# A graph layer on one core: the last four plain quads summed by equality matrix, the last round's units on both PSUM rings

## The chip, the core and the metric

The kernel runs on one core of a Trainium2 chip. A core has five engines that run side by side and meet through semaphores: PE (TensorE, matmuls into PSUM; PEld is its loading of weights), DVE (VectorE), ACT (ScalarE), POOL (GpSimd) and SP (SyncE, which here only issues DMAs). Each engine takes its instructions in the order in which they stand in its queue. The metric is the device time of one execution in microseconds.

## The reference

A graph network layer with 6250 nodes of 128 features and 200000 edges. `src` is the node that an edge is summed into, `dst` the node that it reads; the edges are sorted by `dst`.

```python
h = jnp.maximum(_layernorm(x, axis=-1), 0.0)
xw = h @ W_in
W_ij = shifted_softplus(f_ij @ W_f1 + b_f1) @ W_f2 + b_f2
W_ij = W_ij * f_ij_cutoff
x_ij = xw[dst] * W_ij
out = jax.ops.segment_sum(x_ij, src, num_segments=6250)
return x + shifted_softplus(out @ W_o1 + b_o1) @ W_o2 + b_o2
```

Here `f_ij` has 20 numbers for each edge and `f_ij_cutoff` one. The sum over edges with the same `src` is what the change is about: the edges are not sorted by `src`, so each must be added to a row that can be anywhere.

## The kernel before

**Quads.** 512 edges, in four chunks of 128, are a quad; there are 391, numbered 0 to 390 (the last has three chunks). For each, PE makes the filter weights `W` and gathers the node rows `xg` with one-hot matmuls, ACT scales the rows by the cutoff (`xc`), and DVE multiplies both to the messages: 128 edges on the partitions, 4 x 128 numbers each.

**Three ways to sum messages by `src`.**

- *Permuted quads* (8, 10, ... 388, 191 of them): the messages are split in bf16 parts, sorted by matmuls with a permutation (`pq` to `mst`), and eight quads together, a *round*, are added to the SBUF table `accT` by matmuls with one-hots of the row (`unit_pe`: `un` from `mst` and the one-hots `so`, L838). A round has four units, one for each 128 slots of the sorted edges; a unit fills four PSUM banks, and `unit_evac` adds them to `accT` on DVE (L849). Edges that don't fit go through an overflow path: `over_row`, `over_eq`, `over_sum` (`orow`, `oeq`, `osum`), one scatter (`os`) for two quads. The last round has 7 quads.
- *Plain quads*: DVE makes an equality matrix of the `src` numbers in each chunk (`eq`, `s1_eq`), PE multiplies it with the messages (`pp`, `s3_pe`), so that all edges of one chunk with the same `src` carry the same sum; ACT copies that to SBUF (`s3_copy`), and indices are made that send all but one of equal rows to a trash row (`s3_idx`, `s3_ji`). Then POOL scatters each chunk with an indirect DMA that adds into DRAM (`acc`).
- *Listed quads*: no equality matrix for the sum. Ahead of time a list is made of those rows that occur more than once in a chunk (`l_eq`, `l_count`, `l_scan` and so on); the messages themselves are scattered, and the doubles go to rows of their own behind the table. Later these rows are loaded (`l_load`), summed by `src` (`over_row`, `l_same`, `l_sum`) and scattered once. A list covers 16 quads, made in groups of four; the last covers what is left.

Of the 200 quads that aren't permuted (`splain`), the first 12 are plain and the other 188 are listed, in 12 lists, the last with 12 quads. `listed` sets these bounds (LB and LE in the code).

**Accumulators.** Four tables in DRAM take the scatters in turn, so that a scatter need not wait for the one before. Table 0 is read back and added to `accT` while the last iterations run (`r0_tp`); scatters from then on go to tables 1 to 3.

**The order of work.** The body is one long program, written out in Python with no loop on the chip: iteration i calls fixed steps for quads i+1 to i-4, and steps put down in a table of hooks, keyed by iteration and point (`AT` gives for each its distance and its point in the iteration). A plain quad q has its equality matrix and its messages in iteration q+1, its sums in q+2, its indices in q+4, and is scattered in q+4; a listed quad is scattered in q+2. The units of the last round stand in iterations 393, 395, 397 and 399. The last list is summed from the iteration of its last quad plus LASTLAG = 5 on, or the next one without a unit.

**PSUM.** There are eight banks, in two rings of four. Ring A holds `z`, `xg` and `W` of the main path, ring B all else: `pp`, `pq`, `po`, `orow`, `osum`, `lsum`, and the units, which need all four banks of it.

**The exit and the tail.** Behind the body stands a test whether some list or gather overflowed. Two small matmuls (`fps`, on ring A, L1362) and four DVE instructions make a flag (`flagi`, L1365 to L1369); every engine loads it (L1372) and branches (L1373); here all engines meet. With these inputs the flag is 0. Instructions written behind the body can stand before others of the body in an engine's queue, and the other way round; the queues quoted below are what the chip gets. Then the tail: for 13 groups of 512 nodes, three accumulator tables are loaded (`ta_in`, L1458) and summed (POOL and DVE), transposed, added to `accT`, and taken through the two output matmuls. The rows of `x` that are added at the end are loaded near the end of the body, and the output bias is added to them on DVE (`x_bias`, 13 instructions, L1171).

Of the kernel before, what the change touches and what calls it, by code (L numbers as in the profile page):

```python
# [7 lines left out]
F32 = mybir.dt.float32  # L8
# [12 lines left out]
P = 128  # L21
# [30 lines left out]
SW = 16  # L52
LEARLY = 8
LLATE = 12
LLAG = 12
LASTLAG = 5
LCAP = 7
LFIRST = 3
LREST = 36
# [16 lines left out]
def tile_gnn(ctx: ExitStack, tc: tile.TileContext, x, fB, cT, srcT, srcr, srci, dstr, win_, wf1, wf2, bias, bo1c, wo1,  # L76
# [26 lines left out]
    rounds = unit_rounds(mpq)  # L103
    uslots = unit_slots(rounds)
    units = {i for us in uslots for i in us}
# [3 lines left out]
    plain = {q: n for n, q in enumerate(splain)}  # L109
    NS = len(splain)  # L110
    LB, LE = listed(NS) if spread else (0, 0)
    CE = min(128, EP // P) if spread else EP // P
    CB = min(4 * NS + 64, EP // P) if spread else 0
# [8 lines left out]
    wend = [splain[LB + SW * w + wsize[w] - 1] for w in range(NW)]  # L122
    wlag = [LLAG] * (NW - 1) + [LASTLAG]
    for w in range(NW):
# [13 lines left out]
    ps = edge.enter_context(tc.tile_pool(name="ps", bufs=2, space=PSUM))  # L138
# [275 lines left out]
    def l_base(w):  # L414
        return ACC_R + P * (NA - 1 - w if w < NA else NA + NW - 1 - w)
# [40 lines left out]
    def l_index(w):  # L456
# [4 lines left out]
        nc.vector.tensor_scalar(row, j, pre, None, op0=ALU.add)  # L461
        oh = sp_.tile([P, P + LCAP + 1], BF16, tag="loh", name="loh", bufs=1)
        nc.vector.tensor_scalar(oh[:, :P + LCAP], iotl, pre, None, op0=ALU.is_equal)
        bad = sp_.tile([P, 4 * SW], F32, tag="lbad", name="lbad", bufs=1)[:, :n]
        nc.vector.tensor_scalar(bad, row, float(P), None, op0=ALU.is_gt)
        nc.vector.scalar_tensor_tensor(bad, j, float(LCAP), bad, op0=ALU.is_gt, op1=ALU.max)
        nc.vector.tensor_scalar(row, row, float(l_base(w) - 1), None, op0=ALU.add)
# [8 lines left out]
    def l_id(w):  # L476
        n0 = 4 * (LB + SW * w)
        jd = lst.pop(("jd", w))
        own = sp_.tile([P, LCAP], F32, tag="lown", name="lown", bufs=1)
        n = 4 * wsize[w]  # L480
        t = wk.tile([P, 4 * SW], BF16, tag="lsel", name="lsel", bufs=1)[:, :n]
        for k in range(LCAP):
            nc.vector.scalar_tensor_tensor(t, jd, float(k + 1), srcT_sb[:, n0:n0 + n], op0=ALU.is_equal,
                                           op1=ALU.mult, accum_out=own[:, k:k + 1])
        two = sp_.tile([P, LCAP, 2], BF16, tag="ltwo", name="ltwo", bufs=1)
        nc.vector.tensor_copy(two[:, :, 0], own)
# [339 lines left out]
    un = {}  # L826

    def unit_pe(r, s):
        ts = []
        for g in range(4):  # L830
            t = ps.tile([P, 512], F32, tag="B", name="un", bufs=4)
            ts.append(t)
        qs = rounds[r]
        for q in qs:
            for k in range(3):
                for g in range(4):
                    v = slice(g * CAP, (g + 1) * CAP)
                    nc.tensor.matmul(ts[g][:, :GN], mp[q]["ms", s][v, k * P:(k + 1) * P], mp[q]["oh"][v],  # L838
                                     start=(q == qs[0] and k == 0), stop=(q == qs[-1] and k == 2))
        un[r, s] = ts  # L840
# [52 lines left out]
    with tc.manual_schedule():  # L893
# [115 lines left out]
        def at(i, point, fn, *a):  # L1009
            hooks.setdefault((i, point), []).append((fn, a))  # L1010

        def put(name, base, fn, *a, busy=()):
            d, point = AT[name]
            i = max(clear(base + d, busy) if busy else base + d, 0)
            at(i, point, fn, *a)
            return i
# [70 lines left out]
        busy = units | {prep_start(g) + k for g in range(1, NG) for k in range(5)}  # L1087
# [85 lines left out]
        if spread:  # L1173
            k = clear(mid + 9, busy, 2)
# [3 lines left out]
            k = clear(NQ - 1, busy, 2)  # L1178
# [25 lines left out]
        for r in range(-(-len(mpq) // RKQ)):  # L1204
# [5 lines left out]
            k = put("rk_count", i, rank_count, r, busy=units)  # L1210
            k = max(k + 1, i + AT["rk_own"][0])
            at(k, AT["rk_own"][1], rank_own, r)
            k = clear(max(k, i + AT["rk_over"][0]), units)
            at(k, AT["rk_over"][1], rank_over, r)
            k = max(k + 1, i + AT["rk_slot"][0])
# [5 lines left out]
        for w in range(NW):  # L1221
            for g in range(wsize[w] // 4):
# [9 lines left out]
                k = put("l_dup", i, l_dup, w, g)  # L1232
# [12 lines left out]
            k = clear(i + AT["l_sum"][0], units)  # L1245
# [4 lines left out]
            k = put("l_int", k, over_int, ("L", w))  # L1250
# [6 lines left out]
        for q in mpq:  # L1257
            put("pm", q, perm_oh, q)
            put("rem1", q, part_rem, q, 1)
            put("rem2", q, part_rem, q, 2)  # L1260
            put("ext", q, part_ext, q)
            if q + 4 in units:
                for s in range(4):
                    at(q + 3, "PE2", permute, q, s)
                for s in range(4):
                    at(q + 3, "PE2", perm_out, q, s)
            else:
                for s in range(4):
                    put(f"p{s}", q, permute, q, s)
                    put(f"o{s}", q, perm_out, q, s)  # L1270
            if mpi[q] % 2 or q == mpq[-1]:
                k = mpq[mpi[q] + 1] if mpi[q] + 1 < len(mpq) else q + 2
                put("over_pe", k, over_pe, q)
                put("over_out", k, over_out, q)
                put("over_idx", q, over_idx, q)
                put("over_dg", q, over_dg, q)
                k = put("over_row", q, over_row, q, busy=units)
                put("over_eq", k, over_eq, q)
                k = put("over_sum", q, over_sum, q, busy=units)
                put("over_copy", k, over_copy, q)  # L1280
                put("over_ji", k, over_ji, q)
                k = put("over_int", k, over_int, q)
                at(k, "S", over_scatter, q)
        last = mpq[-1]
        for r, us in enumerate(uslots):
            for s, k in enumerate(us):
                for h in range(3):
                    d, point = AT[f"so{h}"]
                    at(max(k + d, us[s - 1]) if s else k + d, point, unit_oh, r, s, h)
                put("unit", k, unit_pe, r, s)  # L1290
                put("evac", k, unit_evac, r, s)
# [81 lines left out]
    with tc.For_i(0, redo, 1):  # L1373
# [8 lines left out]
        with tc.For_i(0, trips, 1) as ci:  # L1382
# [39 lines left out]
            e = wk.tile([P, P], F32, tag="a", name="fe")  # L1422
# [15 lines left out]
            s = wk.tile([P, P], F32, bufs=1, tag="dg", name="fs")  # L1438
# [126 lines left out]
def unit_rounds(qs):  # L1565
    return [qs[r:r + RND] for r in range(0, len(qs), RND)]
# [23 lines left out]


def listed(ns):
    return (ns - LLATE - (ns - LEARLY - LLATE) // SW * SW) // 4 * 4, ns // 4 * 4


def unit_its(qs):
# [3 lines left out]
def clear(i, busy, n=1):  # L1600
    while any(i + k in busy for k in range(n)):
        i += 1
    return i
# [11 lines left out]
def prep_start(g):  # L1615
    busy = unit_its(sorted_quads(4 * PREP_GAP * (g + 8)))
    return clear(7 + PREP_GAP * (g - 1), busy, 2) - 1
# [100 lines left out]
```

## Time and profile before

| What | us |
|---|---|
| Three runs | 1917.09, 1922.52, 1920.89 (median 1920.89) |
| The profiled execution, its own time | 1917.92 |
| Its span in the profile | 1916.1 |
| PE busy | 1802.2 (94%) |
| DVE busy | 1655.1 (86%) |
| POOL busy | 1516.2 (79%) |
| ACT busy | 1475.0 (77%) |
| The first matmul of the last round's units starts at | 1839.03 |
| The last evacuation of a unit starts at | 1862.71 |
| The first load of the tail is issued at | 1866.01 |

Times within the execution are counted from the start of the span; the profiled execution's own time is 1.8 us more than its span. A busy PE is not a PE at its peak, since matmuls overlap. A line number is that of the kernel file; where several steps share a line, the names of the tiles tell them apart (`osum<-mo,oeq` is a matmul into `osum`). Some records of matmuls can be missing from a trace.

### The profile page before, as it was taken

How to read it: one execution, taken by the hardware profiler on the slowest of the kernel's cores; microseconds unless marked ns; L12 is line 12 of the kernel's file. 1: busy time of each engine (PE TensorE's matmuls, PEld its weight loads, DVE VectorE, ACT ScalarE, POOL GpSimd, SP SyncE). 2: the span in 40 equal slices, each digit the busy share in tenths (PEclk: the TensorE clock that was granted, in tenths of full speed). 3: DMA queues.
4: the chain of work that ended last, by engine and by line, in shares of the span. 5: the costliest groups of instructions: out<-in, count | busy, mean ns of one | idle time of the engine just before them, and what ended most of it. 6: DMA issues, size and time to landing. Idle time of an engine off the chain costs nothing. (4 is left out here: it accounts for less than half of the span.)

```text
span 1916.1 us, 58074 instructions
## 1 busy us (share of the span) xinstructions
PE 1802.2 (94%) x20601; PEld 1220.0 (64%) x20601; DVE 1655.1 (86%) x4692; ACT 1475.0 (77%) x4045; POOL 1516.2 (79%) x964
## 2 busy tenths in 40 slices
PE   3589999999999999999999999999999999999976
PEld 2456666666666666666666666666666666666654
DVE  5678899899999999999999889889889889898766
ACT  3578887778887878887887887887887787787725
POOL 3568777788887888888888888888888888888755
PEclk9799999999999999999999999999999999999997
DMA  7887786777776677776777767667667667667658
GB/s 268 200 178 163 150 194 123 137 129 126 141 134 122 117 139 127 131 144 127 128 132 126 129 116 136 123 118 132 123 121 130 122 125 128 121 114 135 109 104 264
DMA packets 351704, 267.56 MB, mean 140 GB/s; under 512 B 96719, under 2 KB 315258, under 8 KB 351410
## 3 DMA queue, kind: packets, MB, share of 16 engines
q1 hardware_dynamic: 218786, 197.43, 35.5%
q0 software_dynamic: 132336, 66.32, 34.8%
q8 instruction: 163, 2.67, 0.6%
q14 instruction: 131, 1.07, 0.2%
q10 hardware_dynamic: 288, 0.07, 0.0%
HBM read 154.65 MB, written 109.00 MB: 138 GB/s over the span
## 5 line engine op out<-in xcount | busy, mean ns | idle before, releaser
L637 POOL DMA_INDIRECT acc<-s,lji x751 | 1214.3, 1617 | 247.7 <-issue 175.5
L742 PE MATMUL pq<-pt,pm 128*128 128x387 bf16 x3056 | 581.8, 336 | 1.3 <-ACT s L595 0.6
L565 ACT ACTIVATE xc<-xg,cb 128x128 f32<-128x128 f32 x1564 | 448.0, 375 | 163.4 <-PE xg L552 142.6
L748 ACT CAST mst<-pq 128x387 bf16<-128x387 f32 x764 | 363.9, 487 | 91.9 <-PE pq L742 65.6
L560 PEld LDWEIGHTS W<-w,a 128*128 128x128 f32 x3128 | 420.3, 195 | 17.0 <-issue 5.9
L742 PEld LDWEIGHTS <-pm 128*128 128x128 bf16 x3056 | 294.0, 98 | 197.2 <-issue 4.0
L838 PE MATMUL un<-so,mst 32*128 32x392 bf16 x9168 | 408.9, 324 | 10.5 <-DVE rank L684 4.2
L560 PE MATMUL W<-w,a 128*128 128x128 f32 x3128 | 418.4, 277 | 0.0
L838 PEld LDWEIGHTS <-mst 32*128 32x128 bf16 x9168 | 245.5, 93 | 148.3 <-issue 19.7
L371 ACT ACTIVATE a<-a,con 128x512 f32<-128x512 f32 x391 | 282.5, 723 | 11.6
L731 DVE TENSOR_TENSOR pt<-pt 128x512 f32<-128x512 f32 x382 | 260.5, 682 | 0.0
L717 DVE TENSOR_SCALAR pm<-iotp,pos 128x576 bf16<-128x576 f16 x764 | 256.0, 395 | 0.0
L366 ACT ACTIVATE a<-z 128x512 f32<-128x512 f32 x391 | 236.4, 605 | 19.2 <-PE z L361 19.2
L849 DVE TENSOR_TENSOR accT<-un,accT 128x392 f32<-128x392 f32 x368 | 182.4, 557 | 62.5 <-PE un L838 33.0
L823 DVE TENSOR_SCALAR so<-iot,mst 128x392 bf16<-128x392 f16 x764 | 217.9, 335 | 1.9 <-PE un L838 1.9
L637 POOL DMA_INDIRECT acc<-os,oji x108 | 178.9, 1657 | 47.3 <-issue 13.9
L575 DVE TENSOR_TENSOR pt<-W,xc 128x512 f32<-128x512 f32 x191 | 131.3, 688 | 57.1 <-ACT xc L565 28.7
L361 PE MATMUL z<-ft,ws 123*128 123x512 bf16 x391 | 153.7, 394 | 27.7 <-DMA ft<-fsd 21.2
L575 DVE TENSOR_TENSOR s<-W,xc 128x512 f32<-128x512 f32 x188 | 128.5, 684 | 43.3 <-ACT xc L565 32.1
L552 PE MATMUL xg<-wn,oh 63*128 63x128 bf16 x1564 | 155.3, 220 | 10.9 <-DVE oh L378 6.5
L549 PE MATMUL W<-b2rep,onesb 64*128 64x512 bf16 x391 | 152.3, 389 | 0.0
L637 POOL DMA_INDIRECT acc<-s,ji x48 | 77.7, 1618 | 67.3 <-ACT ji L618 27.8
(215 smaller groups left out, 1787.5 us busy)
## 6 DMA issues: line engine op xcount, KB each, us to landing
rb<-reld SPq DMA_DIRECT2D x391, 64.0 KB
sb<-src SPq DMA_DIRECT2D x192, 128.0 KB
fsd<-f SPq DMA_DIRECT2D x49, 480.0 KB
ft<-fsd SPq DMA_DIRECT2D x195, 120.0 KB
fb<-in_fB_dram SPq DMA_DIRECT2D x49, 320.0 KB
ft<-fsd SPq DMA_DIRECT2D x195, 80.0 KB
wn<-tab SPq DMA_DIRECT2D x782, 15.8 KB
acc<-s,lji POOLq DMA_INDIRECT x751
```

The costliest lines, as they stand in the source:

```text
L366: nc.scalar.activation(a, st[q]["z"], AF.Exp)
L371: nc.scalar.activation(a, a, AF.Ln, bias=half, scale=0.5)
L560: nc.tensor.matmul(W[:, c, :], st[q]["a"][:, c * P:(c + 1) * P], w2, start=False, stop=(c == 3))
L565: nc.scalar.mul(xc[:, c, :], st[q]["xg"][:, c, :], late["c", q // CQ][:, 4 * (q % CQ) + c:4 * (q % CQ) + c + 1])
L575: nc.vector.tensor_tensor(m[:, :, :P], st[q]["W"], st[q]["xc"], op=ALU.mult)
L637: nc.gpsimd.indirect_dma_start(out=accs[k][:rows, :], out_offset=bass.IndirectOffsetOnAxis(ap=ji, axis=0), in_=s, in_offset=None, compute_ ...
L717: nc.vector.tensor_scalar(pm[:, c], iotp, rk[r]["pos"][:, 4 * j + c:4 * j + c + 1], None, op0=ALU.is_equal)
L731: nc.vector.tensor_tensor(pt[:, :, k * P:(k + 1) * P], a, high(a), op=ALU.subtract)
L742: nc.tensor.matmul(t[:, :PW], mp[q]["pm"][:, c, s * P:(s + 1) * P], high(mp[q]["pt"][:, c:c + 1, :PW])[:, 0], start=(c == 0), stop=(c == 3))
L748: nc.scalar.copy(mp[q]["ms", s][:, :PW], mp[q].pop(("q", s))[:, :PW])
L823: nc.vector.tensor_scalar(so, iotw[:, :GN], w[:, 3 * P // 2:3 * P // 2 + 1], None, op0=ALU.is_equal)
L838: nc.tensor.matmul(ts[g][:, :GN], mp[q]["ms", s][v, k * P:(k + 1) * P], mp[q]["oh"][v], start=(q == qs[0] and k == 0), stop=(q == qs[-1] a ...
```

## The change

```diff
+LTAIL = 4
...
     def unit_pe(r, s):
         ts = []
         for g in range(4):
-            t = ps.tile([P, 512], F32, tag="B", name="un", bufs=4)
+            t = ps.tile([P, 512], F32, tag="A" if r == len(rounds) - 1 and s % 2 else "B", name="un", bufs=4)
             ts.append(t)
...
                 k = put("over_row", q, over_row, q, busy=units)
-                put("over_eq", k, over_eq, q)
-                k = put("over_sum", q, over_sum, q, busy=units)
+                e = put("over_eq", k, over_eq, q)
+                k = clear(max(e, q + AT["over_sum"][0]), units)
+                at(k, AT["over_sum"][1], over_sum, q)
...
 def listed(ns):
-    return (ns - LLATE - (ns - LEARLY - LLATE) // SW * SW) // 4 * 4, ns // 4 * 4
+    return (ns - LLATE - (ns - LEARLY - LLATE) // SW * SW) // 4 * 4, ns // 4 * 4 - LTAIL
```

The last four of the quads that aren't permuted, 385, 387, 389 and 390, are plain instead of listed. The last list ends with quad 383 and has 8 quads in two groups; its sum starts in iteration 388 instead of 396. The second and fourth unit of the last round take their four banks from ring A, whose tiles of the main path are done by then. The overflow sum is put no earlier than its equality matrix.

The changed kernel has two more lines ahead of the exit, so L1171 there is L1172, and L1372 is L1374.

The order of DVE's queue changes at the exit. Before, from the evacuation of the third unit to the branch (`so` are one-hots for a unit, `xl` and `ft` rows of x, `ojd` indices):

```order
L849 TENSOR_TENSOR accT<-un,accT 128x392 x4
L823 TENSOR_SCALAR so<-iot,mst 128x392 x3
L1171 TENSOR_TENSOR xl<-xl,bo2b 128x512
L535 TENSOR_SCALAR ojd<-idl,con 128x1
L536 SCALAR_TENSOR_TENSOR ojd<-os,con,ojd 128x1
L1171 TENSOR_TENSOR xl<-xl,bo2b 128x512
L849 TENSOR_TENSOR accT<-un,accT 128x392 x4
L1171 TENSOR_TENSOR xl<-xl,bo2b 128x512
L1372 TENSOR_LOAD flagi
L1373 COMPARE_AND_BRANCH
```

With the change, from the evacuation of the last unit:

```order
L850 TENSOR_TENSOR accT<-un,accT 128x392 x4
L1172 TENSOR_TENSOR xl<-xl,bo2b 128x512 x6
L1172 TENSOR_TENSOR ft_118<-ft_118,bo2b 128x512
L1172 TENSOR_TENSOR xl<-xl,bo2b 128x512
L1172 TENSOR_TENSOR ft_120<-ft_120,bo2b 128x512
L1172 TENSOR_TENSOR xl<-xl,bo2b 128x512
L1172 TENSOR_TENSOR ft_122<-ft_122,bo2b 128x128
L1367 TENSOR_REDUCE flag_40286<-fps 1x1
L1368 TENSOR_TENSOR flag_40286<-flag_40286,zcol 1x1
L1370 TENSOR_SCALAR flagi<-flag_40286 1x1
L1371 TENSOR_SCALAR flagi<-flag_40286 1x1
L1374 TENSOR_LOAD flagi
```

Before, ten of the thirteen additions to x stand behind the branch, and the flag is made ahead of the first unit's evacuation; now all stand ahead of the branch, and the flag is made last.

PE's queue before, in iteration 391, near the end of the body (`rtp` is table 0 on its way to `accT`, `lsum` the sum of a list):

```order
L1129 MATMUL lps<-zcol,onesf 128x1
L1145 MATMUL rtp<-idt,r0t 128x128
L796 LDWEIGHTS oeq
L796 MATMUL osum<-mo_112,oeq 128x132
L797 LDWEIGHTS oeq
```

And with the change:

```order
L1130 MATMUL lps<-zcol,onesf 128x1
L1146 MATMUL rtp<-idt,r0t 128x128
L525 MATMUL lsum<-lm,leq 128x128 x4
L526 MATMUL lsum<-con,leq 128x1
L797 LDWEIGHTS oeq
L797 MATMUL osum<-mo_112,oeq 128x132
```

The sum of the last list moves here from behind the third unit, and its row (`orow<-ldg`) from behind the second unit to iteration 388. The sums `pp` of the four quads, four matmuls each, come in iterations 387, 389, 391 and 392, all ahead of the first unit. The two matmuls of the flag (`fps`) move from behind the second matmul of the first unit to behind the last matmul of the last.

POOL's last scatters before, ahead of its branch (`lji` and `ji` are the indices of listed and plain quads, `os` the sums of overflow rows and lists):

```order
L637 DMA acc_78<-s,lji 6912x128
L637 DMA acc_76<-os,oji 6400x128
L637 DMA acc_77<-os,oji 6400x128
L637 DMA acc_78<-os,oji 6400x128
L637 DMA acc_76<-os,oji 6400x128
L1372 TENSOR_LOAD flagi
```

And with the change:

```order
L638 DMA acc_78<-s,ji 6400x128
L638 DMA acc_76<-os,oji 6400x128
L638 DMA acc_77<-s,ji 6400x128
L638 DMA acc_78<-s,ji 6400x128
L638 DMA acc_76<-s,ji 6400x128
L638 DMA acc_77<-os,oji 6400x128
L638 DMA acc_78<-os,oji 6400x128
L638 DMA acc_76<-os,oji 6400x128
L1374 TENSOR_LOAD flagi
```

The number of scatters is the same; three chunks of quad 390 now stand between the sums.

## The prediction

> **What bounds the kernel now.** I read first how busy each engine is in stretches of 5 us (columns: stretch, its length, then for PE, PEld, DVE, ACT and POOL the busy us and the count of instructions, then granted clock, DMA share, GB/s):
>
> ```profile
> 1815.00:1820.00 5.00, 5.00 (x42) 3.81 (x41) 5.00 (x14) 4.59 (x15) 4.09 (x4) 1.00 0.41 42
> 1820.00:1825.00 5.00, 5.00 (x41) 3.32 (x39) 4.55 (x14) 4.16 (x11) 3.99 (x3) 1.00 0.40 40
> 1825.00:1830.00 5.00, 4.49 (x94) 2.73 (x95) 2.88 (x9) 1.41 (x3) 3.36 (x3) 1.00 0.40 34
> 1835.00:1840.00 5.00, 4.98 (x43) 2.78 (x45) 3.52 (x13) 3.58 (x11) 4.09 (x3) 1.00 0.81 189
> 1845.00:1850.00 5.00, 4.11 (x83) 2.43 (x81) 2.65 (x11) 0.00 (x0) 2.62 (x3) 1.00 0.52 92
> ```
>
> Up to 1840 PE sets the pace, and what is added to it there is paid. After that no engine is full. The timeline of the end shows why (start, length, engine, line, operation, in brackets the idle time before it and what ended it):
>
> ```profile
> 1843.27 1.98 DVE L849 TENSOR_TENSOR accT<-un,accT 128x392 f32<-128x392 f32 x4 [1.62 <-PE un L838]
> 1843.88 0.22 PE L796 MATMUL osum<-mo,oeq 128*128 128x132 bf16 x1 [0.67 <-DVE accT L849]
> 1844.57 0.58 PE L838 MATMUL un<-so,mst 32*128 32x392 bf16 x2
> 1845.17 0.77 DVE L823 TENSOR_SCALAR so<-iot,mst 128x392 bf16<-128x392 f16 x3
> 1846.25 3.64 PE L838 MATMUL un<-so,mst 32*128 32x392 bf16 x81 [0.63 <-DVE oeq L790]
> 1849.78 1.98 DVE L849 TENSOR_TENSOR accT<-un,accT 128x392 f32<-128x392 f32 x4 [1.89 <-PE un L838]
> 1856.34 1.98 DVE L849 TENSOR_TENSOR accT<-un,accT 128x392 f32<-128x392 f32 x4 [1.89 <-PE un L838]
> 1862.71 1.98 DVE L849 TENSOR_TENSOR accT<-un,accT 128x392 f32<-128x392 f32 x4 [2.05 <-PE un L838]
> 1864.62 0.68 DVE L1171 TENSOR_TENSOR xl<-xl,bo2b 128x512 f32<-128x512 f32 x1
> 1866.01 20.75 SPq L1458 DMA_DIRECT2D ta_in<-acc  x30
> 1867.14 3.10 DVE L1171 TENSOR_TENSOR xl<-xl,bo2b 128x512 f32<-128x512 f32 x5 [1.84 <-issue]
> 1872.56 0.28 DVE L1171 TENSOR_TENSOR ft<-ft,bo2b 128x128 f32<-128x128 f32 x1
> 1876.56 0.69 DVE L1470 TENSOR_TENSOR ta_in<-ta_in 128x512 f32<-128x512 f32 x1 [3.72 <-POOL ta_in L1464]
> ```
>
> The four units of the last round take turns with their evacuations: some 6.5 us from one L849 to the next, of which the 84 matmuls of a unit need 84 x 3.64 / 81 = 3.8 and the evacuation 2.0. Then comes the exit: all engines meet at the branch (L1373), and only behind it do the loads of the tail start, at 1866.01. From there to the end both kernels run the same code, so the change is worth what it moves that 1866.01. The waits of SP at the branch (us in total, times, longest), and from the chain of waits when the last of them was over:
>
> ```profile
> SPq L1373 <- DMA acc<-os,oji: 2.4, 1, 2.4
> SPq L1373 <- DVEq L1373: 0.6, 1, 0.6
> 1865.47 0.02 SPq L1373
> ```
>
> The last scatter landed first; DVE came 0.6 us behind it, and set the exit.
>
> **The change part by part.** *Four plain quads, in the stretch that PE bounds.* Quads 385, 387, 389 and 390 are now summed by an equality matrix. The early plain quads show each operation (durations min/median/max in ns, first and last start, shape), and the timeline what one quad takes of PE, what a group of the list does, and how full the DMA engines were early on (a row of the first view):
>
> ```profile
> L595 ACT COPY s<-pp x24: 356/377/388, 41.2 to 134.0; 128x258 f32<-128x258 f32 x24
> L406 DVE TENSOR_TENSOR eq<-sb,srcT_sb x24: 405/416/442, 33.0 to 128.5; 128x256 f32<-128x256 int16 x24
>   DMA sb<-src: 5.7, 2
> 0.00:50.00 50.00, 17.06 (x93) 12.47 (x93) 26.23 (x77) 17.54 (x42) 18.35 (x34) 1.00 0.79 272
> 41.77 1.06 PE L587 MATMUL pp<-m,eq 128*128 128x129 f32 x8
> 42.84 0.39 PE L669 MATMUL rkp<-G,trib 128*128 128x512 bf16 x1
> 1676.34 0.55 PE L430 MATMUL lcnt<-wgtb,eql 128*128 128x1 bf16 x16
> 1676.76 0.27 PE L782 MATMUL orow<-unit,mo 128*128 128x128 bf16 x2
> ```
>
> PE pays 42.84 - 41.77 = 1.07 us a quad; beside bf16 matmuls that can overlap it I take 1.0, so 4.0 for the four. Against it the last list has one group less: the 16 matmuls of L430, 1676.76 - 1676.34 = 0.4. DVE gets 2 x 0.42 and ACT 2 x 0.38 us a quad. In the 15 us from 1815 DVE has 2.6 free and ACT 4.8, and before 1840 another 1.5 and 1.4: nothing. Without that cover it would be 3.3 on DVE. The source rows are loaded four iterations ahead; two of the early equality matrices waited 5.7 us for theirs together, but the DMA share was 0.79 then and is 0.4 here, and I take nothing (at most 2.9 for one).
>
> *The last list is summed earlier.* Its row and sum matmuls leave the gaps between the units for the stretch that PE bounds:
>
> ```profile
> 1850.49 0.46 PE L785 MATMUL orow<-ldg,onesf 128*128 128x128 f32 x2 [0.60 <-issue]
> 1856.96 1.16 PE L524 MATMUL lsum<-lm,leq 128*128 128x128 f32 x8 [0.51 <-DVE accT L849]
> ```
>
> They ran while DVE evacuated and cost nothing; now 0.46 and 1.16, less some overlap, 1.4. Its four loads, with which SP waited for the last list scatters, go ahead of the loads of x, and no one waits for either. So unit 0 ends 4.0 - 0.4 + 1.4 = **5.0 us later**. Bounds: 0, if all of it falls into waits, and 6.5, if nothing overlaps and the ring of four banks, which now takes six more tiles, adds half a us twice.
>
> *Units on both rings.* Counted from the first evacuation (1843.27): PE still waits for two banks, for osum and orow, so unit 1 starts at 1.3 as now (1844.57); but it then runs through on the other ring and ends at 5.1 (now 6.5). Unit 2 stands behind osum and the copy that frees its bank, an estimated 0.8, and ends at 9.7 (now 13.1). Unit 3 starts at once; 48 of its matmuls last to 11.9; its last three one-hots stand behind the evacuation on DVE, which ends at 11.7, and take 0.26 each (0.77 for three), so the last 12 matmuls end near 13.6 (now 19.4). **5.8 us gained.** Bounds: 3, if units go on waiting for one-hots, and 8, if PE runs three units without a gap (11.4).
>
> *The exit.* The flag's matmul, fps, takes its bank from the ring that unit 3 now holds, and stands behind it. On DVE the four instructions of the flag come after all additions to x (L1171), of which ten now run behind the branch. No one in the tail needs those early: DVE's first sum there is at 1876.56. So the ten, 1867.14 to 1872.84, become 5.7 us ahead of the exit. Behind the flag, every engine waits with its own load of it, and behind that the whole tail; now these are done early (first two rows: begin of the flag and what follows it):
>
> ```profile
> 1839.93 0.15 DVE L1365 TENSOR_REDUCE flag<-fps 1x1 f32<-1x7 f32 x1
> 1840.43 0.30 DVE L823 TENSOR_SCALAR so<-iot,mst 128x392 bf16<-128x392 f16 x1
> L1372 DVEq TENSOR_LOAD <-flagi x1: 547/547/547, 1862.8 to 1862.8; - x1
> ```
>
> The flag takes 0.5 and the load 0.55. For signal and branch between them no row stands alone; it lies between nothing and the 0.7 that the meeting takes now (last L1171 over at 1865.30, loads at 1866.01), and I take half, 0.35. Together **7.1 us lost**; bounds 6.7 and 7.5.
>
> *The edit of over_sum* takes the later of two iterations, and that is the one it had. No row moves by it.
>
> Sum: 5.0 - 5.8 + 7.1 = **+6.3 us**. The profiled execution took 1917.92 (span 1916.1, and 1.8 around it) and would take 1924.2. It was a fast one: the three runs have a median of 1920.89, and all four known times a mean of 1919.6. From that mean I predict 1919.6 + 6.3 = **1926**. 0.3% of it, about what a measurement of this kernel can tell from no change, is 5.8 us; the forecast lies just beyond.
>
> **The rivals.** *Not slower: the work added to PE falls into waits.* If the iterations of the four quads are paced by the exchange between PE, ACT and DVE, the 5.0 goes and +1.3 is left: 1921, no change. For it, PE is free for 0.5 us in 1825 to 1830; against it, it has 5.00 of 5.00 before. The loop must have 4 us of waits from 1810 to 1840 for this to decide.
>
> *POOL comes last at the exit.* A listed quad is scattered two iterations after its own, a plain one four. From quad 387 on, 15 scatters follow each other (rows of POOL's timeline; the row between is the idle time, us and times, of early plain scatters behind earlier ones):
>
> ```profile
> 1834.45 1.54 POOL L637 DMA_INDIRECT acc<-s,lji  x1 [0.30 <-DVE flagi L1370]
> 1836.30 1.56 POOL L637 DMA_INDIRECT acc<-s,lji  x1 [0.30 <-issue]
>   DMA acc<-s,ji: 26.8, 16
> 1859.01 2.04 POOL L637 DMA_INDIRECT acc<-os,oji  x1 [5.49 <-ACT oji L812]
> 1861.35 1.54 POOL L637 DMA_INDIRECT acc<-os,oji  x1 [0.30 <-POOLq L1373]
> ```
>
> One takes 1836.30 - 1834.45 = 1.85 us. If 387's come when 389's do now, and 2 us later for the longer loop, at 1836.5, the 15 end at 1864.3. The last landed 3.5 us after its start (1861.35 to 0.6 before 1865.47), which gives 1866.3; DVE will need until 1843.3 + 5.0 + 13.6 + 2.0 + 6.3 + 0.5 = 1870.7. But the 48 early scatters waited 26.8 us for earlier ones, 0.56 each: 8.4 for 15, hence 1874.7, and the exit comes 10 us later than now: 1930. It decides from 0.3 us of waiting for each. Against it: then one or two accumulators took turns, here three.
>
> [...]
>
> *The units stay in step with DVE.* One-hots, row comparisons and evacuations share DVE. If each unit waits for them, 3 us are gained instead of 5.8: +9.1, 1929.
>
> **How the numbers follow.** Forecast 0.46 (its own range 1923 to 1929), additions in waits 0.22, POOL last 0.2, units in step 0.07, something unseen that makes it faster 0.05. Slower are half of the forecast and nearly all of POOL and units, 0.48; faster 0.07, with a little of the second case; the same 0.45. The range goes from below the second case, 1918, to beyond POOL's, 1933.
>
> **What would show it.** Eight-row groups of L588 near 1810 to 1845 that put the first evacuation 5 us later; evacuations some 5.1, 4.6 and 3.9 apart; eleven L1172 between the last evacuation and the flag; DVE as the last that SP waits for at the branch; the tail's first load 6 us later. The prediction is wrong if that load is not later (PE had room, or the units gain more), or if SP's last wait there is a scatter.

## The result and the profile after

The changed kernel takes 1923.55 us, median of 12 runs (1919.65 to 1926.55), and the kernel before 1919.09, median of 12 beside them. The ratio is 1.0023, 95% interval 1.0012 to 1.0033: 4.4 us (2.3 to 6.3) slower. The prediction was +6.3 us and 1926, from 1918 to 1933. A difference of 4.4 us is under the 0.3% that the prediction set for "the same", although the interval leaves out zero. The profiled execution took 1921.22 us, with a span of 1919.4.

The busy time in stretches, as in the prediction's first view (PE, PEld, DVE, ACT, POOL, then clock, DMA share, GB/s):

```profile
1815.00:1820.00 5.00, 5.00 (x42) 3.62 (x41) 4.96 (x16) 4.73 (x15) 0.00 (x0) 1.00 0.24 69
1820.00:1825.00 5.00, 4.92 (x40) 3.05 (x42) 3.97 (x14) 4.25 (x13) 3.90 (x3) 1.00 0.28 23
1825.00:1830.00 5.00, 5.00 (x104) 3.54 (x97) 2.95 (x8) 0.60 (x3) 3.54 (x2) 1.00 0.32 30
1835.00:1840.00 5.00, 5.00 (x33) 3.26 (x33) 2.58 (x9) 3.91 (x12) 4.08 (x3) 1.00 0.53 107
1845.00:1850.00 5.00, 4.34 (x94) 2.46 (x89) 4.29 (x13) 0.27 (x1) 2.80 (x3) 1.00 1.14 328
```

PE is as full as before until 1840, so what was put there had to be paid. POOL has no scatter begun in 1815 to 1820, because the quads that were scattered there are plain now and scattered later. The timeline of the end:

```profile
1845.18 1.99 DVE L850 TENSOR_TENSOR accT<-un,accT 128x392 f32<-128x392 f32 x4 [2.02 <-PE un L839]
1846.48 3.66 PE L839 MATMUL un<-so,mst 32*128 32x392 bf16 x84
1850.17 1.98 DVE L850 TENSOR_TENSOR accT<-un,accT 128x392 f32<-128x392 f32 x4 [0.69 <-PE un L839]
1850.35 6.05 PE L839 MATMUL un<-so,mst 32*128 32x392 bf16 x132
1854.30 1.98 DVE L850 TENSOR_TENSOR accT<-un,accT 128x392 f32<-128x392 f32 x4
1856.75 1.68 PE L839 MATMUL un<-so,mst 32*128 32x392 bf16 x36 [0.35 <-DVE so L824]
1858.44 1.98 DVE L850 TENSOR_TENSOR accT<-un,accT 128x392 f32<-128x392 f32 x4
1860.34 3.69 DVE L1172 TENSOR_TENSOR xl<-xl,bo2b 128x512 f32<-128x512 f32 x6
1866.56 0.15 DVE L1367 TENSOR_REDUCE flag<-fps 1x1 f32<-1x7 f32 x1
1869.86 9.77 SPq L1460 DMA_DIRECT2D ta_in<-acc  x16
```

The four evacuations are now 5.0, 4.1 and 4.1 us apart (before 6.5, 6.6, 6.4). The third and the fourth begin without a wait of DVE: the last two units are no longer what DVE waits for. Then eleven additions stand ahead of the flag, and the tail's first load comes 11.4 us after the last evacuation instead of 3.3. What SP waits for at the branch, in us:

```profile
SPq L1374 <- DVE flagi L1371: 21.0, 1, 21.0
```

It is DVE's flag, and no scatter. Behind the flag (first value the duration in ns, then the start), before and after:

```profile
L1373 POOLq INC_SWDGE_SEM  x1: 910/910/910, 1861.3 to 1861.3; - x1
```

```profile
L1374 DVEq TENSOR_LOAD <-flagi x1: 543/543/543, 1867.1 to 1867.1; - x1
L1375 POOLq INC_SWDGE_SEM  x1: 909/909/909, 1868.0 to 1868.0; - x1
```

POOL has a step of its own of 0.91 us at this branch. Before, POOL had done it while DVE was still waiting for the fourth unit; now it starts when the flag has been loaded, ends at 1868.9, and lies on the way from there to the tail's first load.

The account by stages, in us, each the distance between two starts in a trace (quad: its first matmul of `W<-b2rep`; evac: the first and the last evacuation of the last round; load: the tail's first load; end: end of the span), for the two kernels and those of the experiments, one profiled execution each:

```
                     quad      quad 385    first to   last evac   load
                     352-364   to evac     last evac  to load     to end
before               54.69     34.53       19.44       3.30       50.09
after                52.23     39.69       13.26      11.42       49.54
units alone          55.58     34.55       17.06      11.41       50.18
list alone           52.33     39.71       21.39       3.29       49.76
list alone, again    52.71     39.71       19.47       3.30       51.73
flag early           52.38     43.48       13.73       8.33       50.15
flag far early       53.30     39.79       13.83       8.44       49.52
units, flag early    55.28     35.17       17.84       3.29       49.94
list row early       54.73     34.35       16.16       3.52       49.61
list row, again      54.70     34.36       15.95       3.29       50.32
last index early     52.62     34.36       15.37       4.07       49.43
no additions         54.70     34.52       17.11       5.79       50.52
```

After against before: -2.5 + 5.2 - 6.2 + 8.1 - 0.6 = +4.1 us, for 4.4 measured. Outside these stretches both kernels run the same code, but for the last list's indices, told of below; two executions drift there by some us either way (up to 6 at quad 300), and those drifts are left out.

### The profile page after: what moved, and what is told of

It is laid out like the page before. It is cut to its first block, busy times and chain, and to the rows that moved or that the text cites. A ratio compares the mean times of both kernels' runs of the same rounds, so it can differ in the third digit from the quotient of the medians.

```text
span 1919.4 us, 58125 instructions
## 1 busy us (share of the span) xinstructions
PE 1800.2 (94%) x20617; PEld 1214.7 (63%) x20617; DVE 1657.4 (86%) x4702; ACT 1475.6 (77%) x4057; POOL 1514.3 (79%) x964
## 5 line engine op out<-in xcount | busy, mean ns | idle before, releaser
L638 POOL DMA_INDIRECT acc<-s,lji x736 | 1191.3, 1619 | 243.6 <-issue 174.5
L561 PEld LDWEIGHTS W<-w,a 128*128 128x128 f32 x3128 | 419.9, 195 | 15.6 <-issue 5.0
L561 PE MATMUL W<-w,a 128*128 128x128 f32 x3128 | 417.6, 277 | 0.0
L839 PEld LDWEIGHTS <-mst 32*128 32x128 bf16 x9168 | 238.8, 93 | 150.0 <-issue 15.5
L638 POOL DMA_INDIRECT acc<-s,ji x63 | 101.7, 1614 | 87.7 <-ACT ji L619 39.4
```

The costliest lines, as they stand in the source:

```text
L561: nc.tensor.matmul(W[:, c, :], st[q]["a"][:, c * P:(c + 1) * P], w2, start=False, stop=(c == 3))
L638: nc.gpsimd.indirect_dma_start(out=accs[k][:rows, :], out_offset=bass.IndirectOffsetOnAxis(ap=ji, axis=0), in_=s, in_offset=None, compute_ ...
```

## The experiments

The theory is that of the prediction with its four terms (loop, units, exit, and now a gain near quad 360 that is larger than foreseen). The rivals: POOL's scatters make the exit late and not the flag; the gain near quad 360 is chance, or the whole price of a group; the parts don't add up.

**Units on both rings alone.**

```diff
-LTAIL = 4
+LTAIL = 0
```

> The units on both rings alone; the four quads stay listed, as in the kernel before. Theory (the flag behind the ten additions sets the exit, and the two parts add up): the loop costs nothing, so the first evacuation starts where it does before. First to last evacuation takes 14.4 us instead of 19.4: as in the changed kernel (13.3), and 1.2 more, because the last list's row and sum stand between the units again. From the last evacuation to the tail's first load it takes 11.4 us as in the changed kernel, instead of 3.3. With 0.5 us less in the tail that is -5.0 + 8.1 - 0.5 = +2.6 us against before. Rival (the late exit comes from the POOL queue, which the four plain quads fill, and not from the flag's place): POOL ends here as early as before, so the exit takes some 3.3 us after the last evacuation and the kernel gains the 5 us of the units.

Measured: 1.0030 of before (1.0017 to 1.0044), +5.8 us. The exit is that of the changed kernel to a hundredth, 11.41 us, although POOL's last scatter began at 1856.57 already: the flag's place makes the exit late, the rival falls. The loop costs nothing. But the units gave 2.4 us and not 5.0. PE's timeline of this kernel:

```profile
1844.94 0.49 PE L786 MATMUL orow<-ldg,onesf 128*128 128x128 f32 x2
1845.53 0.74 PE L839 MATMUL un<-so,mst 32*128 32x392 bf16 x3
1848.03 3.64 PE L839 MATMUL un<-so,mst 32*128 32x392 bf16 x81 [1.75 <-DVE leq L519]
```

The last list's row takes a bank of ring B between the second and the third unit. It comes free when DVE has made the equality matrix `leq`, and that stands behind an evacuation. So the third unit waits 1.75 us. The part of the change that moves the list is what makes the other ring worth its price: each of the two parts alone is slower than before, and together they cost less than the sum.

**The four plain quads alone.**

```diff
-            t = ps.tile([P, 512], F32, tag="A" if r == len(rounds) - 1 and s % 2 else "B", name="un", bufs=4)
+            t = ps.tile([P, 512], F32, tag="B", name="un", bufs=4)
```

> The four plain quads alone; all units stay on ring B, so the flag is made ahead of the first unit's evacuation again and ten additions to x stand behind the branch. Theory: the loop ends 5.1 us later by the added matmuls and 2.4 us earlier by the third group of the last list that is gone near 1690 us, the first evacuation thus 2.7 us later than before; first to last evacuation 19.4 us as before, since the list's row and sum that leave the gaps ran beside evacuations; exit 3.3 us as before. +2.7 us against before. Rival 1 (the 2.4 us near 1690 are chance): +5.1 us. Rival 2 (units were held up by the list's row and sum): about +1.2 us.

Measured: 1.0014 (1.0003 to 1.0024), +2.7 us as expected, but not by the terms expected: in the profiled execution the stages add up to -2.36 + 5.18 + 1.95 - 0.01 - 0.33 = +4.43 us, so that the numbers agree is in part luck. The loop's 5.2 and the 2.4 near quad 360 are there to a tenth. The units took 21.4 us, 2.0 more than before, and the matmuls of two of them ran slower. First PE's timeline, then three stretches around the first of the two (the value after the five engines is the granted clock):

```profile
1846.96 5.32 PE L839 MATMUL un<-so,mst 32*128 32x392 bf16 x81 [0.63 <-DVE oeq L791]
1854.50 3.64 PE L839 MATMUL un<-so,mst 32*128 32x392 bf16 x81 [0.15 <-DVE accT L850]
1860.14 5.32 PE L839 MATMUL un<-so,mst 32*128 32x392 bf16 x81 [0.15 <-DVE accT L850]
```

```profile
1844.00:1846.00 2.00, 1.18 (x8) 0.57 (x8) 2.00 (x5) 0.27 (x1) 0.97 (x1) 1.00 1.09 346
1846.00:1848.00 2.00, 1.36 (x21) 0.78 (x24) 1.81 (x7) 0.00 (x0) 1.54 (x1) 0.83 1.17 331
1848.00:1850.00 2.00, 2.00 (x32) 1.24 (x28) 0.58 (x3) 0.00 (x0) 1.39 (x1) 0.50 0.95 211
```

The 81 matmuls of the second unit took 5.32 us, with the clock at 0.50 from 1848 to 1850, those of the third 3.64, as in the kernel before at a clock of 1.00, and those of the fourth 5.32 again. So it was run again:

> The four plain quads alone, a second look. In the first one the four units took 21.4 us instead of 19.4, and two of them ran for some 4 us at a granted clock of 0.50 (5.3 us for 81 matmuls instead of 3.64). If that comes from the change (less work of PE in the gaps between the units), it is there again; if it was chance, the units take some 18 to 19.4 us, at full clock.

```profile
1848.73 5.32 PE L839 MATMUL un<-so,mst 32*128 32x392 bf16 x81 [0.77 <-DVE oeq L791]
1861.55 3.64 PE L839 MATMUL un<-so,mst 32*128 32x392 bf16 x81 [0.15 <-DVE accT L850]
```

The second unit ran at half clock again (0.50 from 1850 to 1852; 8.3 us from the first evacuation to the second, where before took 6.5), the fourth did not, and the four took 19.5 us. One of the two dips comes back, the other does not. The wait of PE just ahead of its 81 matmuls, 0.63 and 0.77 us, is hardly longer than in the kernel before (0.63), which kept its clock at 1.00; why it drops here is not settled.

**The flag made in the body.** Its three steps are hooks now, and its tile no longer stands behind the last unit.

```diff
-    (dmax, flagf, fps, flag1 and flagi behind the loop)
+        at(390, "D2", flag_own)
+        at(392, "PE2", flag_sum)
+        at(393, "D0", flag_max)
```

> The changed kernel with the flag made inside the body (own part in iteration 390, sum in 392, maximum in 393), so its tile no longer stands behind the last unit, and ten of the additions to x stand behind the branch as in the kernel before. Theory A (only the flag's place makes the exit late): the tail's first load comes 3.3 us after the last evacuation (1858.4), at 1861.8, 8 us earlier than in the changed kernel: 3.6 us faster than before. Theory B (with the flag gone, the scatters of the plain quads end last): the last scatter started at 1863.36 in the changed kernel, some 0.5 us of it because additions ran beside the last ones; from 1862.9, 3.5 us to its landing and 0.6 to the load give 1867.0, only 2.9 us earlier than in the changed kernel: +1.5 us against before, and SP waits last for a scatter. I expect B.

Measured: 1.0012 (0.9997 to 1.0027), +2.3 us. The exit is 8.3 us: neither 3.3 nor 11.4, as theory B has it. But the loop took 3.8 us longer, from one badly placed instruction (timeline, then four stretches):

```profile
1832.75 1.78 DVE L1299 TENSOR_REDUCE dmax<-dropT 128x1 f32<-128x1568 bf16 x1
1834.79 1.16 PE L525 MATMUL lsum<-lm,leq 128*128 128x128 f32 x8 [2.07 <-DVE zcol L1134]
1836.64 2.08 PE L561 MATMUL W<-w,a 128*128 128x128 f32 x8
```

```profile
1833.00:1835.00 2.00, 0.21 (x1) 0.21 (x2) 2.00 (x6) 0.00 (x0) 0.37 (x1) 1.00 0.63 147
1835.00:1837.00 2.00, 2.00 (x19) 1.70 (x19) 1.01 (x5) 0.90 (x4) 0.00 (x0) 0.83 0.95 279
1837.00:1839.00 2.00, 2.00 (x10) 1.62 (x10) 0.17 (x1) 1.54 (x6) 1.22 (x1) 0.50 0.00 0
1839.00:1841.00 2.00, 2.00 (x13) 1.37 (x12) 1.71 (x5) 0.95 (x3) 1.70 (x2) 0.82 0.37 33
```

The reduction on DVE stands ahead of `zcol`, PE waits for that 2.07 us (0.23 in the changed kernel), and behind the wait it runs at half clock, 0.50 from 1837 to 1839: eight matmuls of L561 take 2.08 us and not 1.16. In this execution the loop is 3.8 us longer, nearly twice the length of the wait. The times of the whole kernel do not bear that out for every execution: the stages of this one add up to +6.0 us against before, beyond the interval of +2.3 (-0.6 to 5.2) that its twelve runs gave. So the reduction went where the kernel before has it:

```diff
-        at(390, "D2", flag_own)
+        at(376, "D2", flag_own)
```

> The changed kernel with the flag made inside the body, its own part now in iteration 376 (in the run before, in 390, its 1.78 us reduction stood ahead of what PE waited for, PE waited 2.07 us and then ran at half clock). Now the loop should end as in the changed kernel, so the first evacuation stands 5.2 us later, counted from quad 385, than before, and the units take 13.3 us. Theory B (POOL's scatters end last once the flag is early): the last scatter starts 17.7 us after the first evacuation as in the changed kernel (1863.36 - 1845.18 is 18.2, less 0.5 of contention with the additions), and the tail's first load 4.0 us later, so 21.7 us after the first evacuation, instead of 24.7 in the changed kernel and 22.7 before: -3 us against the changed kernel, +1.4 against before. Theory A (only the flag's place): 13.3 + 3.3 = 16.6 us after the first evacuation, 8 us faster than the changed kernel.

Measured: 1.0010 (0.9996 to 1.0023), +1.9 us. The loop is back at 39.8 us, 3.7 less than in the run before, while the measured time fell by only 0.4. The end of this kernel (timeline, then SP's waits):

```profile
1859.84 1.98 DVE L850 TENSOR_TENSOR accT<-un,accT 128x392 f32<-128x392 f32 x4 [0.45 <-PE un L839]
1864.23 1.54 POOL L638 DMA_INDIRECT acc<-os,oji  x1 [0.30 <-issue]
1868.28 11.55 SPq L1471 DMA_DIRECT2D ta_in<-acc  x19
```

```profile
SPq L1386 <- DMA acc<-os,oji: 13.3, 2, 10.2
```

Theory B holds: from the first evacuation to the load it takes 22.3 us (expected 21.7), and SP waits for the last scatter. That one began 18.2 us behind the first evacuation, as in the changed kernel, and not 0.5 sooner. In the changed kernel the late flag hid a second late thing only 2.4 us shorter, the queue of scatters that the plain quads fill. Taking the flag out of the way alone doesn't give back the 8 us.

**Units on both rings, the flag early, the four quads listed.** This is the kernel with the units alone, with the three hooks of the flag at 390, 392 and 393.

> Units on both rings, the flag made inside the body, and the four quads listed as before: the change without its costs. If the three steps (loop, units, exit) add up, the loop costs nothing, the last evacuation starts 5.0 us earlier than before, near 1857.8, the list's sum is scattered last, near 1858, lands 3.5 us later, and the tail's first load comes at about 1862.2 instead of 1866.0: -3.8 us against before, 8 us faster than the changed kernel. If POOL's queue or the list's sum holds the exit where it is, no more than -1 us.

Measured: 1.0002 (0.9989 to 1.0015). The exit is 3.29 us again, against 11.41 with the late flag: here, where POOL is done early, the flag's place is worth the 8.1 us. The gain expected in all, -3.8, is missed since the units took 17.8 us, with the third one's wait for `leq` (1.75 us) in them, where 14.4 were expected, and the loop 0.6 more.

**The ten additions left out** of the kernel with the units alone (one execution, 1917.10 us; rows of the output lack the bias):

```diff
-        for g in range(len(tgroups)):
+        for g in range(3):
             at(mpq[-1] + (10 if g < 10 else 7) + g, "D2", x_bias, g)
```

> Units on both rings alone, and ten of the thirteen additions to x left out (those that ran ahead of the flag; the bias is missing in these rows of the output). It divides the 11.4 us from the last evacuation to the tail's first load. If the additions are worth their 5.9 us and the rest is the late flag itself (0.5), its load on every engine (0.5), POOL's step at the branch (0.9) and the branch, 11.4 - 5.9 = 5.5 us are left; if the additions only cover another wait, more than 7.

```profile
1860.89 0.68 DVE L1172 TENSOR_TENSOR xl<-xl,bo2b 128x512 f32<-128x512 f32 x1
1861.49 0.15 DVE L1367 TENSOR_REDUCE flag<-fps 1x1 f32<-1x7 f32 x1
1864.78 14.86 SPq L1460 DMA_DIRECT2D ta_in<-acc  x23
```

The exit takes 5.79 us. So of the 8.1 us the additions are 11.41 - 5.79 = 5.6, and 2.5 are the flag, its load, POOL's step and the branch, one behind the other.

**The list's row earlier**, to be rid of the wait for `leq`; the rest as in the kernel with units and early flag, its own part in iteration 376:

```diff
+            j = i - 2 if w == NW - 1 else i
-            at(i, "L", l_start, w)
-            put("l_dg", i, l_dg, w)
-            at(i, "PE2", over_row, ("L", w))
-            put("l_same", i, l_same, w)
+            at(j, "L", l_start, w)
+            put("l_dg", j, l_dg, w)
+            at(j, "PE2", over_row, ("L", w))
+            put("l_same", j, l_same, w)
```

> Units on both rings, the flag made early (own part in iteration 376), the four quads listed; and the row of the last list two iterations earlier, between the first and the second unit. With the row behind the second unit, the third unit waited 1.75 us for the list's equality matrix on DVE, which stands behind an evacuation. If that wait is all that kept the units apart, first to last evacuation takes 17.8 - 1.75 + 0.3 (one more tile ahead of the second unit) = 16.4 us instead of 19.4 before; with the exit at 3.3 us and no cost in the loop that is -3.0 us against before: 1916, faster than both kernels. If the wait moves to another bank of the ring, -1 us.

Measured: 0.9984 (0.9973 to 0.9996), 3.1 us faster than before. The units take 16.2 us (expected 16.4), and PE no longer waits for `leq`. That confirms the reading of the wait, though the terms were larger than foreseen on both sides: against the kernel with the row in its old place (17.84 us), the third evacuation follows the second 2.5 us sooner (1.75 expected), and the second follows the first 0.8 later (0.3 expected).

**The gain near quad 360.** The stage table has it in all kernels with the short list (52.2 to 53.3 us from quad 352 to quad 364), and with the long one in the last alone, told of below (elsewhere 54.7 to 55.6). DVE's and PE's timeline before shows the largest part of it:

```profile
1685.30 0.21 DVE L472 TENSOR_TENSOR lji<-lrow,srcT_sb 128x48 int32<-128x48 f32 x1
1686.92 0.68 DVE L575 TENSOR_TENSOR pt<-W,xc 128x512 f32<-128x512 f32 x1
1687.66 0.38 PE L361 MATMUL z<-ft,ws 123*128 123x512 bf16 x1 [1.34 <-DVE pt L575]
```

and DVE's and PE's after:

```profile
1647.76 0.19 DVE L473 TENSOR_TENSOR lji<-lrow,srcT_sb 128x32 int32<-128x32 f32 x1
1682.30 0.39 PE L362 MATMUL z<-ft,ws 123*128 123x512 bf16 x1
```

The indices of the last list (L461 to L473, ten small instructions, 1683.6 to 1685.6) stand ahead of the product `pt` that PE waits for. With two groups instead of three they are due 38 us earlier, where PE waits for nothing of DVE's. Is it that move, or the group that is gone? The last kernel keeps the third group, but moves its work and the block four listed quads ahead:

```diff
-                n = LB + SW * (w - 1) + 4 * g - LSHIFT
+                n = LB + SW * (w - 1) + 4 * g - (4 if w == NW - 1 else 0)
```

> The kernel of the list's early row (units on both rings, early flag, four quads listed), and the groups of the last list counted four listed quads earlier, so that the block of small DVE instructions that gives its indices stands near 1647 us, as in the kernels with a list of 8, instead of 1683.6 to 1685.5, where PE waited 1.34 us behind it for a product on DVE. Theory (the four plain quads saved time near 1690 because this block moved, not because a group is gone): the gain from quad 352 to quad 364, 2.0 to 2.5 us in three kernels with the shorter list (1.4 in a fourth), comes here too but for the 0.4 us of the group's matmuls: 1.3 to 2.0 us against the same kernel without the shift. The end stays as it was: 1.3 to 2 us faster than that kernel, some 4.8 us faster than before. Rival (the third group's own work was the cost, wherever it stands): no gain from quad 340 to 364.

> The same without the shift, beside it on the same chip: 3.1 us faster than before, as in its first run; no gain from quad 352 to 364.

```profile
1645.04 0.21 DVE L473 TENSOR_TENSOR lji<-lrow,srcT_sb 128x48 int32<-128x48 f32 x1
```

Measured on the same chip: 0.9961 (0.9948 to 0.9974) with the shift, 7.5 us faster than before, and 0.9976 (0.9962 to 0.9989) without it. From quad 352 to quad 364 it takes 52.62 against 54.70 us: 2.1 gained, more than the 1.3 to 2.0 expected. But the third group's own work has left this stage too. Its 16 matmuls stand ahead of quad 352 now, with those of the group before it:

```profile
1563.14 0.95 PE L431 MATMUL lcnt<-wgtb,eql 128*128 128x1 bf16 x32
```

From quad 300 to quad 364, a stretch that holds them in both kernels, the gain is 1.5 us, within what was expected; but two executions of the same code drift there by as much, and the intervals of the two measured times overlap. Quad by quad, before against after, 1.40 of the 2.5 us stand in the quad in which PE waited for `pt`, 0.40 in the one with the 16 matmuls, and 0.49 in the one ahead of it. So the larger part of the gain comes from the place of the block; up to 0.9 us is the group's own work, and this kernel doesn't tell the two apart. At 1911.15 us against 1917.87 it is faster than the kernel before, which the changed one is not.

## Why the prediction was right, and where not

**The exit** was the step on which the forecast rested, and its mechanism is shown: the flag behind the additions, DVE last, the load late. It was 8.1 us and not 7.1. The ten additions have the size given (5.6 for 5.7). What stands behind the flag was undersized, 2.5 for 1.4: I took the branch for 0.35 and left out POOL's step of 0.91 us, which the trace of before shows at 1861.3, hidden.

**The loop**: +5.2 for 4.0 + 1.4 = 5.4. It is 5.2 to 5.3 in four executions with the list's change (in the fifth the flag disturbs it), and within 0.2 of nothing in those without (0.6 in the one whose flag is made at 390). In the changed kernel the products of the four quads were 0.9, 1.0, 1.0 and 0.9, less a wait of 0.45 that fell away, and the list's row and sum 0.22 and 1.53. PE had no room, so the first rival falls.

**The list's group** is the term that failed. It was put down as the 0.4 us of L430; it is 2.5 in the changed kernel (1.4 to 2.4 in the four other executions with the short list), mostly since the group's end sets when the block of indices comes, and that block kept PE waiting 1.34 us. The row with that wait stands in the trace of before; the prediction looked at the end alone, and at PE's matmuls of the group, not at what DVE had to do behind them.

**The units**: 6.2 gained for 5.8. The ends, counted from the first evacuation, were forecast at 5.1, 9.7 and 13.6, and the evacuations began at 5.0, 9.1 and 13.3. The last one-hots of the fourth unit waited for DVE as foreseen (0.35 us). That the gain depends on the list's move (2.4 without it) was not said.

**The tail** was 0.6 shorter; the prediction called it the same code, which it is, and the 0.6 is no more than the drift of executions. Before, additions ran beside POOL's first sum there, which took 1.75 us and takes 1.26 now. But a tail without additions is not always the shorter one: it took 50.18 us with the units alone and 50.52 with ten additions left out, against 50.09 before.

**POOL last** (the rival of 1930) did not happen, and its price per scatter was too high: the last scatters began 1.84 to 2.00 us apart, nearly all without a wait:

```profile
1859.52 1.54 POOL L638 DMA_INDIRECT acc<-os,oji  x1 [0.30 <-issue]
1861.36 1.69 POOL L638 DMA_INDIRECT acc<-os,oji  x1 [0.30 <-DMA acc<-s,ji]
1863.36 2.09 POOL L638 DMA_INDIRECT acc<-os,oji  x1 [0.31 <-issue]
```

But it is the second in line, as the run with the flag far early shows. There the last scatter, with no addition beside it, took 1.54 us and not 2.09. In the changed kernel the one at 1859.52, with an addition beside no more than its last 0.72 us, took 1.54 too, and the two behind it, which ran beside additions from start to end, took 1.69 and 2.09: 0.15 and 0.55 us more, with POOL still ahead of DVE.

With the group at its 2.5 instead of 0.4 the forecast of +6.3 would have been +4.2, against +4.4 measured; the other errors (an exit that costs 1.0 more, units and tail that gain 1.0 more) cancel, which is luck. So the time lies inside the range and the forecast's own range of 1923 to 1929, near its lower end, and the difference on the near side of what was called a change, to which the prediction gave 0.45 against 0.48 beyond it.

## What to carry to other kernels

A tile that is taken last from a shared ring puts its reader behind everything that holds the ring (here the flag behind the last unit: with the units on both rings alone 11.4 us from the last evacuation to the load, and 3.3 with the flag early); before moving tiles to a "free" ring, ask who takes a bank there next and what is queued on that engine by then. When work leaves a list, price not only its instructions but when the block behind it now comes due: here the same block kept PE waiting 1.3 us at one place, and not at all 38 us earlier. And when the last of several engines at a meeting is sped up, look up the second: its distance is the whole gain (here 2.4 us, where the flag's place alone was worth 8.1).

## What the runs showed of the hardware

**A wait of 2 us on PE was followed by half clock.** Behind the wait of 2.07 us the clock was at 0.50 to 0.83 from 1835 to 1841, and the loop took 3.8 us longer in that one execution. The wait of 1.75 us for `leq` was not followed by it: with the units alone the 81 matmuls behind it took 3.64 us, and there as well as with units and early flag the third evacuation came 3.93 us behind the start of `leq`. With gaps of no more than 0.8 us each ahead of the second unit the clock went to 0.50 as well, at the same place in both executions with the four plain quads alone. What sets it off is not shown: PE was busy for 1.18 + 1.36 of the 4 us at whose end the clock fell in the first of them, and for 1.44 + 1.27 in the second, but the kernel before kept its clock at 1.00 with 1.33 + 1.33 of 4 us (1842 to 1846).

**Each engine's load of the flag took 0.45 to 0.54 us** in the changed kernel, and with the units on both rings alone the tail's first load came 5.79 us behind the last evacuation even with the ten additions left out, against 3.3 where flag, load and POOL's step were done ahead of time.
